# T3 on GpSimd, S's sums moved, the second sum split: a modulated 1-D convolution chain

## The chip, the cores and the metric

The kernel runs on one core of a Trainium2 chip. The metric is the device time of one execution in microseconds; the median of the runs is taken. The engines are TensorE (PE in the profile), VectorE (DVE), ScalarE (ACT), GpSimd (POOL) and SyncE (SP), which issues most of the DMAs.

## The reference

128 samples, each with 64 channels and 1024 positions, pass through four layers of a convolution with three taps whose weights depend on the sample. The layers are "same", "upsample", "same" and "downsample" with a fixed blur, there is no nonlinearity between them, and the input is added at the end.

```python
def _layer(x, style, w, b, mw, mb, typ):
    s = style @ mw.T + mb
    weight = SCALE * w * s[:, None, :, None]
    demod = lax.rsqrt(jnp.sum(weight * weight, axis=(2, 3)) + EPS)
    weight = weight * demod[:, :, None, None]
    if typ == 'same':
        out = jax.vmap(_conv_same)(x, weight) + b[None, :, None]
    elif typ == 'upsample':
        out = jax.vmap(_conv_up)(x, weight.transpose(0, 2, 1, 3)) + b[None, :, None]
        out = _blur(out, 2.0 * blur_k, (1, 1))
    elif typ == 'downsample':
        xb = _blur(x, blur_k, (2, 2))
        out = jax.vmap(_conv_down)(xb, weight) + b[None, :, None]
    return out
for i, typ in enumerate(('same', 'upsample', 'same', 'downsample')):
    out = _layer(out, style, weights[i], biases[i], mod_w[i], mod_b[i], typ)
x = x + out
```

## The kernel before

Since nothing nonlinear stands between the layers, the kernel multiplies the four weights of a sample into one filter of nine taps and runs that over the sample once. The three positions at either end, where the borders count, are computed apart and spread over the loop as one-off work.

Four samples (two pairs, of which one half lies on the upper and one on the lower 64 partitions) make one iteration q, 32 in all. The filter of nine taps over three planes (positions modulo three) is done with five products in place of nine taps by nine: conv0 to conv4 on TensorE, each 12 matmuls of 340 columns in float32. Their moving operands are sums of planes of the input X: T0 and T4 (`in04`, VectorE), T1 and T2 (`in1`, `in2`; one tile T12, made by GpSimd in the steady loop, lines L727 and L732 of the profile), T3 (`in3`, L712). T1, T2, T0 and T4 come from a tile G that VectorE makes with `in_g2` and `in_g01` (L663 with G in its name). Their weights are W (three stages of small matmuls) and H, sums of taps of W (`combine_a`, `combine_b`, `residual`: L663 with H, L660).

The products go into PSUM: conv3, then conv1 and conv2, then conv0 into psA(q), and conv4 into a bank pair Y that is one for all iterations. Between them stand sums on VectorE: `sum1` (y from psA and m3, a copy of conv3's result that ACT makes), `sum2` (Y = 3 m3 + psA after conv2, then y minus psA). conv4 adds onto Y, so it follows the first step of `sum2`.

The weights of later iterations are made in the same loop: `stage1` makes S(q+4), `stage2` makes R(q+2) with a scaled copy by ACT (table C), `stage3_b` and `stage3_a` make W(q+2). In the iterations 5 to 27 a part of stage2 is shared (`share`): it needs sums on S (`share_sums`, L463). The last group of `stage3_b` needs sums on R (`r_sums`, L589). Both are one `tensor_add` of 128 x 256 on VectorE with both inputs in SBUF.

The schedule is written out by hand: each engine gets its instructions in the order in which the functions are called, and semaphores are set between engines where data is handed on. `early_turn` writes iterations 0 to 3, `turn_of` 4 to 28 (4 is the entry, with an order of its own), and straight code the last three. In `turn_of(q)`, n is q+1, c is q+2 and s is q+4; its first half ends before conv4(q), its second half belongs to the time from conv4(q) to conv4(q+1). `EXTRA` holds the one-off work by iteration (`small_rest`, `var_newton`, tables on GpSimd in 5 and 7, and from 8 on `setup_x`, `rest0`, `rest1`, `rest1_bias`, `rest2` and `blur_side` on VectorE), `SLOTS` one-off matmuls in 9, 12, 14 and 19.

X has two buffers. SP's queue issues the six loads of an iteration (`load`, L146) and the stores of the outputs (`store`, L834) in the order of the calls; a load waits until the readers of its buffer are done.

Of the kernel before, what the change touches and what calls it, by code (L numbers as in the profile page):

```python
# [63 lines left out]
def kernel(  # L64
# [18 lines left out]
    nc_v, nc_a, nc_g = nc.vector, nc.scalar, nc.gpsimd  # L83
# [57 lines left out]
    def load(q, planes=slice(0, 3)):  # L141

        if q < NQ:
            at = slice(planes.start * PL, planes.stop * PL)
            for c in range(2):
                nc.sync.dma_start(Xs[q % NX][:, c, at], x[2 * q + c, :, at])  # L146
# [17 lines left out]
    def unit(pool, name):  # L164

        if pool is ps_w:
            return [pool.tile([P, 512], F32, tag=f"u{r}", name=f"{name}_{r}") for r in range(2)]
        t = pool.tile([P, 2, 512], F32, tag="u", name=name)
        return [t[:, r, :] for r in range(2)]


    NB = 340
    Y = ps_y.tile([P, 2, 512], F32, name="Y")
# [287 lines left out]
    def share_sums(q):  # L461
        t = whole[q]
        nc_v.tensor_add(t[:, :, 6:8], t[:, :, 1:5:3], t[:, :, 2:6:3])  # L463
# [92 lines left out]
    def new_w(q):  # L556
        Wq[q] = (
            wf_pool.tile([P, 9, 2, C], F32, tag="Wf", name=f"Wf{q}"),
            wf_pool.tile([P, 3, K, 2, C], F32, tag="H", name=f"H{q}"),
        )  # L560
# [5 lines left out]
    def blocks(ps, at):  # L566
        return [b.rearrange("c (a o) -> c a o", o=C)[:, at, :] for b in ps]

    def same_row(dst, weight, t, slots, first=False, last=False):
        for r, rows in enumerate(HALF):  # L570
            for c, cols in enumerate(HALF):
                nc.tensor.matmul(  # L572
                    dst[r][cols],
                    weight[rows],
                    t[rows, c, slots, :],
                    start=first,
                    stop=last,
                    skip_group_check=True,
                )

    def stage3_out(q, ps, at, n, engs=(nc_a, nc_a)):
        W = Wq[q][0]
        for r in range(2):
            src = ps[r][:, : n * C].rearrange("c (a o) -> c a o", o=C)
            scaled_copy(engs[r], W[:, at : at + n, r], src, t0[:, q, r : r + 1])

    def r_sums(q):
        t = chain[q]
        nc_v.tensor_add(t[:, :, 7:9], t[:, :, 2:6:3], t[:, :, 3:7:3])  # L589
# [38 lines left out]
    def stage3(q, part, pool=None, engs=(nc_a, nc_a)):  # L628

        t = chain[q]  # L630
        ps = unit(pool or ps_w, f"psW{q}_{part}")
        if part == 0:
            new_w(q)
        kinds = ((0, 1), (2,))[part]
        n = 0
        for i, kind in enumerate(kinds):
            for k in range(K):
                gs = [g for g in range(K) if 0 <= K * g + kind - k < 7]
                lo, m = gs[0], len(gs)
                first = K * lo + kind - k  # L640
                n += 1
                step = len(kinds)
                at = slice(i + step * lo, i + step * (lo + m - 1) + 1, step)
                same_row(
                    blocks(ps, at),
                    w0s[kind][:, k, :],
                    t,
                    slice(first, first + K * (m - 1) + 1, K),
                    n == 1,
                    n == K * len(kinds),  # L650
                )
        stage3_out(q, ps, *((3, 6), (0, 3))[part], engs)
        return ps
# [8 lines left out]
    def sum_of(out, x, f, y, op=ALU.add):  # L662
        nc_v.scalar_tensor_tensor(out, x, f, y, op0=ALU.mult, op1=op)  # L663
# [6 lines left out]
    def combine_a(q):  # L670

        chain.pop(q)
        a, b, c, h1, h2, h3 = taps(q)
        sum_of(h1, c, -2.0, a)
        residual(q)
        sum_of(h3, h1, 1.0 / 6.0, b)
# [9 lines left out]
    NJ = NB + 2  # L686
# [4 lines left out]
    BOTH_PAIRS = slice(0, 2)  # L691
    PAIR = slice(0, 1), slice(1, 2)

    def plane(buf, i, pairs=BOTH_PAIRS):

        at = PL * (2 - i) if i < 3 else PL * 2 + 1
        return buf[:, pairs, at : at + NJ]

    def t_tile(q, tag):
        if (q, tag) not in Ts:  # L700
            Ts[q, tag] = tpool.tile([P, 2, 1 + (tag != "T3"), PL], F32, tag=tag, name=f"{tag}_{q}")
        return Ts[q, tag]
# [3 lines left out]
            Gs[q] = gpool.tile([P, 2, 3 * PL], F32, tag="G", name=f"G{q}")  # L706
        return Xs[q % NX], Gs[q]

    def in3(q, pairs=BOTH_PAIRS):
        if q < NQ:  # L710
            X, t = Xs[q % NX], t_tile(q, "T3")
            nc_v.tensor_sub(t[:, pairs, 0, :NJ], plane(X, 3, pairs), plane(X, 1, pairs))  # L712

    def in_g01(q, pairs=BOTH_PAIRS):
        if q < NQ:
# [27 lines left out]
    def product(q, m, ps, groups=range(K)):  # L743

        W, H_ = Wq[q]
        tag, i = SLOT[m]
        for g in groups:
            for s, rows in enumerate(HALF):
                for c, cols in enumerate(HALF):
                    if m in (0, 4):  # L750
                        w = W[rows, tap(m // 2, g), c, :]
                    else:
                        w = H_[rows, m - 1, g, c, :]
                    nc.tensor.matmul(  # L754
                        ps[s][cols, :NB],
                        w,
                        Ts[q, tag][rows, c, i, g : g + NB],
                        start=(g == 0 and m == 3),
                        stop=(g == K - 1),
                        skip_group_check=True,  # L760
                    )
# [4 lines left out]
    m3c, y1w = {}, {}  # L766

    def parts(q):

        if isinstance(A[q], list):  # L770
            return [(slice(s, s + 1), A[q][s][:, None, :NB]) for s in range(2)]
        return [(slice(0, 2), A[q][:, :, :NB])]

    def banks(q):
        return A[q] if isinstance(A[q], list) else [A[q][:, s] for s in range(2)]
# [3 lines left out]
    def open_a(q):  # L779
        A[q] = ps_conv.tile([P, 2, 512], F32, tag="u", name=f"psA{q}")  # L780
        return banks(q)
# [22 lines left out]
    def conv2(q, *groups):  # L804
        product(q, 2, banks(q), groups or range(K))

    def sum2(q, steps=(0, 1)):
        for s, a in parts(q) if 0 in steps else ():
            sum_of(Y[:, s, :NB], m3c.pop(q)[:, s], 3.0, a)
        for s, a in parts(q) if 1 in steps else ():  # L810
            nc_v.tensor_sub(y1w[q][:, s], y1w[q][:, s], a)  # L811

    def conv4(q, *groups):
        product(q, 4, Y_banks, groups or range(K))

    def conv0(q, *groups):
        product(q, 0, banks(q), groups)
# [453 lines left out]
    def extra(*at):  # L1271
        EXTRA.get(at, lambda: None)()
# [4 lines left out]
    def sharing(q):  # L1277
        return FIRST < q < NQ - 4
# [105 lines left out]
    def turn_of(q):  # L1384
        n, c, s = q + 1, q + 2, q + 4
        entry = q == FIRST
        stage2(c)
        r_sums(c)
        if not entry:
            conv2(q)  # L1390
        sum2(q)
        if entry:
            conv4(q)
        stage3_b(c, open_a(n))
        combine_a(n)
        if entry:
            conv0(q, 0, 1)
        else:
            conv4(q)
        stage3_a(c)  # L1400
        combine_b(n)
        conv3(n)
        if entry:
            copy_m3(n)
        outputs(q, 2)
        for i in range(3):
            load(c + 1, slice(i, i + 1))
        if s < NQ:
            stage1_a(s)
        else:  # L1410
            slot(ends3, 3, unit(ps_w, "psE"), 3)
        if not entry:
            copy_m3(n)
        in04(n)
        in3(c)
        if q in SMALL:
            l, bs = SMALL[q]
            nc_v.memset(high(bs.stop - bs.start), 0.0)
        in_g2(c)
        conv0(q, *((2,) if entry else range(K)))  # L1420
        if entry:
            conv1(n, 0, 1)
        outputs(q, 1)
        if s < NQ:
            stage1_b(s)
            in_g01(c)
        else:
            rest3()
        if sharing(q):
            share(c + 1, banks(q))  # L1430
            share_copy(c + 1)
        outputs(q, 0)
        if q in SLOTS:
            slot(*SLOTS[q], Y_banks)
        if q in SMALL:
            small(q)
        conv1(n, *((2,) if entry else range(K)))
        sum1(n)
        if s == NQ:
            in_g01(c)  # L1440
        if sharing(q + 1):
            share_sums(s)
        in1(c, nc_g)
        in2(c, nc_g)
        for i in range(3):
            extra(q, i)
        if s + 1 < NQ:
            scale3(s + 1)

# [5 lines left out]
    q, n, c = NQ - 3, NQ - 2, NQ - 1  # L1455
    stage2(c)
    conv2(q)
    stage3(c, 0)
    sum2(q, (0,))
    combine_a(n)  # L1460
# [28 lines left out]
    q, n = NQ - 2, NQ - 1  # L1489
# [21 lines left out]
    q = NQ - 1  # L1511
# [89 lines left out]
```

## Time and profile before

| | |
|---|---|
| median of 3 runs | 511.38 us (509.64 to 512.12) |
| profiled execution | 514.02 us, of which the span is 512.2 us |
| mean granted TensorE clock | 0.989 |
| PE / DVE / ACT / POOL busy | 94% / 86% / 61% / 29% |
| instructions | 26699 |

The profile is of one execution. "Busy" is the union of an engine's instructions; a line gives its source line, the tiles it writes and reads, how often it ran, and in brackets the idle time of its engine just before it with what ended that. L663 is a helper (`sum_of`), so its rows are told apart by tiles. A row of a stretch of time gives the busy time and count of PE, PEld, DVE, ACT and POOL in it, then the granted clock, the DMA share and GB/s. L754 rows are two records per matmul.

### The profile page before, as it was taken

What the parts mean: (1) busy time and instruction counts of PE and PEld (TensorE: products, weight loads), DVE (VectorE), ACT (ScalarE), POOL (GpSimd) and SP (SyncE); (2) the same over time, 40 slices, a digit from 0 to 9 for tenths busy, and PEclk for the clock granted to TensorE, in tenths of its full rate; (3) what the DMA queues carried; (4) which work ended last, traced back from release to release, by engine and by line L of the source; (5) the groups of instructions that cost most, each with busy time, mean ns of one, the idle gap of its engine ahead of it and who ended that gap; (6) DMA issues with size and microseconds to landing.
All of it is one profiled execution on the core that took longest, in us unless ns stands there. A gap on an engine that the chain in (4) does not pass through costs nothing. (4 is left out here: it accounts for less than half of the span.)

```text
span 512.2 us, 26699 instructions
## 1 busy us (share of the span) xinstructions
PE 481.8 (94%) x11928; PEld 372.7 (73%) x11928; DVE 441.3 (86%) x684; ACT 313.3 (61%) x718; POOL 147.3 (29%) x173
## 2 busy tenths in 40 slices
PE   8999999898999999899999999999999999999975
PEld 7877888566997766776798767789666666688732
DVE  5799987679899889997979999869999999887784
ACT  5566577265666567556667665667665676765422
POOL 2433341333134322132333222333122333212200
PEclk9999999899899999999999999999999999999989
DMA  7207363055244455334554433455344555434514
GB/s 238 86 24 243 110 232 107 9 167 167 79 140 136 152 169 153 87 125 142 167 168 160 127 107 131 150 167 160 100 135 130 150 169 165 134 118 130 168 58 164
DMA packets 50499, 70.72 MB, mean 138 GB/s; under 512 B 5648, under 2 KB 47312, under 8 KB 50384
## 3 DMA queue, kind: packets, MB, share of 16 engines
q1 hardware_dynamic: 49792, 68.32, 42.4%
q8 instruction: 94, 1.54, 1.3%
q10 hardware_dynamic: 592, 0.69, 0.4%
q14 instruction: 21, 0.17, 0.1%
HBM read 35.36 MB, written 33.62 MB: 135 GB/s over the span
## 5 line engine op out<-in xcount | busy, mean ns | idle before, releaser
L754 PE MATMUL psA<-T,H 64*64 64x340 f32 x2304 | 190.2, 449 | 3.4 <-DVE y L663 3.2
L754 PEld LDWEIGHTS psA<-T,H 64*64 64x64 f32 x2304 | 100.5, 134 | 45.1 <-issue 7.4
L446 POOL TENSOR_TENSOR S<-S 128x128 f32<-128x128 f32 x28 | 23.4, 835 | 230.3 <-ACT S L361 230.3
L663 DVE SCALAR_TENSOR_TENSOR G<-X 128x1376 f32<-128x1376 f32 (+2 forms) x65 | 78.8, 1215 | 0.2 <-DMA X<-in_x 0.2
L754 PE MATMUL Y<-T,Wf 64*64 64x340 f32 x768 | 65.0, 460 | 5.4 <-DVE Y L663 5.3
L727 POOL TENSOR_TENSOR T<-G 128x684 f32<-128x684 f32 x28 | 46.6, 1663 | 75.3 <-DVE G L663 53.4
L361 ACT ACTIVATE R<-psR,tC 128x448 f32<-128x448 f32 x63 | 36.6, 631 | 46.1 <-PE psR L468 26.2
L754 PE MATMUL psA<-T,Wf 64*64 64x340 f32 x768 | 64.5, 446 | 0.0
L361 ACT ACTIVATE psW<-psA 128x128 f32<-128x128 f32 x100 | 19.3, 268 | 70.0 <-PE psA L572 60.5
L361 ACT ACTIVATE Wf<-psW,t 128x256 f32<-128x256 f32 (+2 forms) x76 | 32.7, 480 | 30.6 <-PE psW L572 30.3
L741 DVE TENSOR_TENSOR T<-G 128x1368 f32<-128x1368 f32 (+1 forms) x33 | 50.6, 1537 | 0.0
L754 PEld LDWEIGHTS Y<-T,Wf 64*64 64x64 f32 x768 | 34.3, 135 | 22.3 <-DVE Y L663 8.9
L732 POOL TENSOR_TENSOR T<-G 128x684 f32<-128x684 f32 x28 | 50.1, 1789 | 0.0
L468 PE MATMUL psR<-S,E 64*64 64x64 f32 (+1 forms) x1472 | 48.4, 237 | 1.3 <-issue 1.3
L572 PEld LDWEIGHTS psA<-R,w0s 64*64 64x64 f32 x1000 | 36.4, 137 | 14.8 <-issue 8.3
L468 PEld LDWEIGHTS psR<-S,E 64*64 64x64 f32 x1472 | 42.1, 134 | 6.1 <-issue 1.8
L572 PE MATMUL psA<-R,w0s 64*64 64x64 f32 (+2 forms) x1000 | 38.4, 268 | 8.5 <-issue 6.4
L390 PEld LDWEIGHTS psS<-wd,w2n 64*64 64x64 f32 x1120 | 37.3, 133 | 11.2 <-ACT S L361 0.8
L754 PEld LDWEIGHTS psA<-T,Wf 64*64 64x64 f32 x768 | 32.5, 133 | 12.2
L829 ACT ACTIVATE o<-psA,tb,td 128x340 f32<-128x340 f32 x63 | 37.2, 651 | 6.4 <-PE psA L754 6.4
L663 DVE SCALAR_TENSOR_TENSOR y<-psA,m 128x680 f32<-128x680 f32 x32 | 27.7, 865 | 13.8 <-PE psA L754 7.5
L829 ACT ACTIVATE o<-Y,tb,td 128x340 f32<-128x340 f32 x63 | 36.7, 638 | 4.6 <-PE Y L754 3.9
(165 smaller groups left out, 883.3 us busy)
## 6 DMA issues: line engine op xcount, KB each, us to landing
out<-o SPq DMA_DIRECT2D x167, 170.0 KB, 4.3
X<-in_x SPq DMA_DIRECT2D x150, 172.0 KB, 3.8
X<-in_x SPq DMA_DIRECT2D x14, 516.0 KB, 5.4
out<-o SPq DMA_DIRECT2D x6, 510.0 KB, 5.8
out<-o SPq DMA_DIRECT2D x2, 340.0 KB, 2.7
Xe<-in_x_ends SPq DMA_DIRECT2D x1, 512.0 KB, 6.7
out<-o ACTq DMA_DIRECT2D x3, 170.0 KB, 3.9
par<-in_params SPq DMA_DIRECT2D x2, 192.0 KB, 3.4
```

Source lines behind the costliest of these rows:

```text
L361: nc_a.activation(dst, src, AF.Copy, scale=f)
L390: nc.tensor.matmul(ps[r][cols, at * C : (at + n) * C], weight[rows], wd[c if r == 0 else 1 - c][rows, taps], start=first, stop=last, skip_ ...
L446: nc_g.tensor_add(t[:, :, 2], t[:, :, 2], t[:, :, 0])
L468: nc.tensor.matmul(dst[r][cols], weight[rows], st[c if r == 0 else 1 - c][rows, slots, :], start=False, stop=last, skip_group_check=True,)
L572: nc.tensor.matmul(dst[r][cols], weight[rows], t[rows, c, slots, :], start=first, stop=last, skip_group_check=True,)
L663: nc_v.scalar_tensor_tensor(out, x, f, y, op0=ALU.mult, op1=op)
L727: eng.tensor_add(t[:, :, 0, :NJ], plane(g, 2), plane(g, 1))
L732: eng.tensor_sub(t[:, :, 1, :NJ], plane(g, 2), plane(g, 1))
L741: nc_v.tensor_sub(t[:, pairs, :, :NJ], both(a, PL), both(b, 1))
L754: nc.tensor.matmul(ps[s][cols, :NB], w, Ts[q, tag][rows, c, i, g : g + NB], start=(g == 0 and m == 3), stop=(g == K - 1), skip_group_check ...
L829: nc_a.activation(dst, src, AF.Identity, bias=add, scale=d3)
```

## The change

- `in3` gets an engine, and the steady loop makes T3(n) on GpSimd in the iteration whose conv3(n) reads it; before, VectorE made T3(c) one iteration earlier. T3(30) is made on GpSimd as well; T3(31) stays on VectorE.
- The loads of X(c+1) are issued at the head of the iteration, behind T3(n), which is the last reader of that buffer; before, behind the stores of conv4's output.
- `share_sums(c+1)` stands behind `in04(n)` and ahead of `in_g2(c)`, in the iteration that uses it; before, `share_sums(s)` stood behind `sum1` in the iteration ahead.
- The first step of `sum2` is two instructions, one for each PSUM bank of Y.
- In the entry iteration `sum2(q)` and conv4(q) stand ahead of `r_sums(c)`.
- The one-off work stands ahead of `in1` and `in2`, which changes the order on GpSimd.

```diff
--- before.py
+++ after.py
@@ -706,10 +706,10 @@
             Gs[q] = gpool.tile([P, 2, 3 * PL], F32, tag="G", name=f"G{q}")
         return Xs[q % NX], Gs[q]
 
-    def in3(q, pairs=BOTH_PAIRS):
+    def in3(q, pairs=BOTH_PAIRS, eng=nc_v):
         if q < NQ:
             X, t = Xs[q % NX], t_tile(q, "T3")
-            nc_v.tensor_sub(t[:, pairs, 0, :NJ], plane(X, 3, pairs), plane(X, 1, pairs))
+            eng.tensor_sub(t[:, pairs, 0, :NJ], plane(X, 3, pairs), plane(X, 1, pairs))
 
     def in_g01(q, pairs=BOTH_PAIRS):
         if q < NQ:
@@ -805,8 +805,10 @@
         product(q, 2, banks(q), groups or range(K))
 
     def sum2(q, steps=(0, 1)):
-        for s, a in parts(q) if 0 in steps else ():
-            sum_of(Y[:, s, :NB], m3c.pop(q)[:, s], 3.0, a)
+        if 0 in steps:
+            m3 = m3c.pop(q)
+            for s, a in enumerate(banks(q)):
+                sum_of(Y[:, s, :NB], m3[:, s], 3.0, a[:, :NB])
         for s, a in parts(q) if 1 in steps else ():
             nc_v.tensor_sub(y1w[q][:, s], y1w[q][:, s], a)
 
@@ -1385,12 +1387,17 @@
         n, c, s = q + 1, q + 2, q + 4
         entry = q == FIRST
         stage2(c)
-        r_sums(c)
-        if not entry:
+        if entry:
+            sum2(q)
+            conv4(q)
+            r_sums(c)
+        else:
             conv2(q)
-        sum2(q)
-        if entry:
-            conv4(q)
+            r_sums(c)
+            sum2(q)
+            in3(n, eng=nc_g)
+        for i in range(3):
+            load(c + 1, slice(i, i + 1))
         stage3_b(c, open_a(n))
         combine_a(n)
         if entry:
@@ -1403,8 +1410,6 @@
         if entry:
             copy_m3(n)
         outputs(q, 2)
-        for i in range(3):
-            load(c + 1, slice(i, i + 1))
         if s < NQ:
             stage1_a(s)
         else:
@@ -1412,7 +1417,8 @@
         if not entry:
             copy_m3(n)
         in04(n)
-        in3(c)
+        if sharing(q):
+            share_sums(c + 1)
         if q in SMALL:
             l, bs = SMALL[q]
             nc_v.memset(high(bs.stop - bs.start), 0.0)
@@ -1438,12 +1444,10 @@
         sum1(n)
         if s == NQ:
             in_g01(c)
-        if sharing(q + 1):
-            share_sums(s)
+        for i in range(3):
+            extra(q, i)
         in1(c, nc_g)
         in2(c, nc_g)
-        for i in range(3):
-            extra(q, i)
         if s + 1 < NQ:
             scale3(s + 1)
 
@@ -1455,6 +1459,7 @@
     q, n, c = NQ - 3, NQ - 2, NQ - 1
     stage2(c)
     conv2(q)
+    in3(n, eng=nc_g)
     stage3(c, 0)
     sum2(q, (0,))
     combine_a(n)
```

## The prediction

> **What bounds the kernel now.** I read the head of the page first (what each engine is busy with), then the groups of instructions by line, then the timeline of one iteration, then the waits of TensorE. Iteration q is counted from the first matmul of conv4(q) to that of conv4(q+1).
>
> ```profile
> span 512.2 us, 26699 instructions
> PE 481.8 (94%) x11928; PEld 372.7 (73%) x11928; DVE 441.3 (86%) x684; ACT 313.3 (61%) x718; POOL 147.3 (29%) x173
> ...
> L712 DVE TENSOR_TENSOR T<-X 128x684 f32<-128x684 f32 x32 | 27.6, 864 | 0.0
> L463 DVE TENSOR_TENSOR S<-S 128x256 f32<-128x256 f32 x23 | 28.9, 1258 | 0.0
> L589 DVE TENSOR_TENSOR R<-R 128x256 f32<-128x256 f32 x25 | 11.5, 461 | 14.8 <-ACT R L361 14.7
> L732 POOL TENSOR_TENSOR T<-G 128x684 f32<-128x684 f32 x28 | 50.1, 1789 | 0.0
> ```
>
> TensorE is busy 94% of the span, VectorE 86%. The two lines L463 (the sums on S) and L589 (the sums on R) are the same instruction on the same shape, 256 elements a partition; one takes 1258 ns and the other 461. Iteration 24 shows why.
>
> ```profile
> 406.21 1.95 PE L754 MATMUL Y<-T,Wf 64*64 64x340 f32 x24 [0.33 <-DVE Y L663]
> 413.26 0.61 DVE L443 SCALAR_TENSOR_TENSOR S<-psS,tB,S 128x128 f32<-128x128 f32 x2 [0.17 <-PE psS L390]
> 413.78 1.58 DVE L663 SCALAR_TENSOR_TENSOR G<-X 128x1376 f32<-128x1376 f32 x1
> ...
> 415.35 0.86 DVE L663 SCALAR_TENSOR_TENSOR y<-psA,m 128x680 f32<-128x680 f32 x1
> 415.53 1.68 POOL L727 TENSOR_TENSOR T<-G 128x684 f32<-128x684 f32 x1 [2.13 <-DVE G L663]
> 416.14 1.35 DVE L463 TENSOR_TENSOR S<-S 128x256 f32<-128x256 f32 x1
> 417.14 1.85 POOL L732 TENSOR_TENSOR T<-G 128x684 f32<-128x684 f32 x1
> 417.24 1.16 ACT L361 ACTIVATE R<-psR,tC 128x448 f32<-128x448 f32 x2 [0.84 <-PE psR L468]
> 417.41 2.60 DVE L1071 TENSOR_TENSOR Ue<-Ve 128x448 f32<-128x448 f32 x2
> 419.56 0.49 PE L572 MATMUL psA<-R,w0s 64*64 64x64 f32 x16
> 419.93 0.41 DVE L589 TENSOR_TENSOR R<-R 128x256 f32<-128x256 f32 x1
> 420.26 0.86 DVE L663 SCALAR_TENSOR_TENSOR Y<-m,psA 128x680 f32<-128x680 f32 x1
> 420.39 0.45 PE L572 MATMUL psA<-R,par 64*64 64x128 f32 x8 [0.35 <-DVE R L589]
> 421.18 1.09 PE L754 MATMUL Y<-T,Wf 64*64 64x340 f32 x12 [0.33 <-DVE Y L663]
> ```
>
> GpSimd's first T12 operation runs from 415.53 to 417.21. The sums on S are asked for at 416.14 and end at 417.49, 0.28 after it. GpSimd's second operation ends at 418.99, 1.50 after the sums, and the two L1071 steps, begun at 417.41, end at 420.01, 1.02 after that. So a VectorE step with two SBUF inputs and a GpSimd operation that reads SBUF run one at a time, and they take turns. The y sum at 415.35 and the Y sum at 420.26, with an input in PSUM, keep 0.86 whatever GpSimd does.
>
> The rest of the iteration is paced by TensorE: before L443 VectorE idles 0.17 for the psS matmuls. The chain that TensorE waits for at the end is G sum (end 415.36), GpSimd, VectorE steps, sums on R, Y sum (end 421.12), conv4 (421.18), with TensorE idle for R and again for Y. This stretch decides the change.
>
> **The change, part by part.** T3 leaves VectorE: 0.864 us an iteration (row L712). That is worth nothing by itself, since it stands ahead of the 0.17 wait for psS: VectorE only waits longer there. S's sums move to the same place, cost about 0.41 there, and that is hidden by the same wait. T3 lands on GpSimd behind the two T12 operations, in the very stretch shown above; the trace has no T3 there, but T12 has its shape (684 elements), so it is priced at one port turn, 1.50, and at most 1.79 (row L732). Below, if it found the port free, it costs nothing.
>
> ```profile
> 172.29 2.73 DVE L973 TENSOR_TENSOR Xm<-Xe,sc 128x512 f32<-128x512 f32 x2
> 206.00:209.00 3.00, 1.27 (x52) 1.15 (x50) 2.97 (x6) 0.00 (x0) 0.00 (x0) 1.00 0.05 14
> 481.06 0.56 DVE L663 SCALAR_TENSOR_TENSOR H<-H,Wf 128x384 f32<-128x384 f32 x1
> ```
>
> With one-off steps on VectorE between the y sum and the sums on R (L1071 here) the turns now go, on iteration 24's times: first T12 to 417.21; first step 0.48 to 417.69; second T12 to 419.19; second step 0.48 to 419.67 (I halve the 1.02, less the pipelining); T3 1.50 to 421.17; sums on R 0.28 to 421.45. It was 420.34. The Y sum is split: 680 elements take 0.86 and 384 take 0.56 (481.06), so 340 take 0.50, and the second half waits for the first (it does in the changed program's instruction list, about 0.03), so 1.03 for 0.86. conv4 waits for the second half in that list, so nothing starts sooner and 0.17 is added. Y ends at 422.40 instead of 421.12, and conv4 comes 1.28 later. Such iterations are 8, 10, 11, 13, 15, 16, 17 and 20 to 24, twelve in all; first and last are L973 (172.29) and L1071 above. Iteration 9 has twelve small steps and I count it too. Where the steps are shorter the rise is a little less: 13 x 1.2 = 15.6. In iteration 10 TensorE is idle 1.73 there already (3.00 less 1.27 in the stretch from 206), until after Y has ended, which hides 0.9. **+14.7.**
>
> ```profile
> 325.26 1.85 POOL L732 TENSOR_TENSOR T<-G 128x684 f32<-128x684 f32 x1
> 326.35 1.16 ACT L361 ACTIVATE R<-psR,tC 128x448 f32<-128x448 f32 x2 [1.82 <-PE psR L468]
> 327.54 0.43 DVE L589 TENSOR_TENSOR R<-R 128x256 f32<-128x256 f32 x1 [1.94 <-ACT R L361]
> ```
>
> Without such steps the sums on R are asked for while the second T12 runs, get the next turn, and T3 follows harmlessly: no change. But in iteration 18 R lands at 327.51, after the second T12 (327.11 here, 0.18 sooner without S's sums). T3 then goes first, to 328.45, and the sums end at 328.73 instead of 327.97: **+0.9** with the split. In 12, 14 and 19 R comes later still and only the split counts, +0.1 each: **+0.3**.
>
> **Iteration 3 to 4.** The Y sum stood behind the sums on R, and those behind ACT; conv4 stood behind the Y sum.
>
> ```profile
> 91.52 1.16 ACT L361 ACTIVATE R<-psR,tC 128x448 f32<-128x448 f32 x2 [2.17 <-PE psR L534]
> 92.71 0.46 DVE L589 TENSOR_TENSOR R<-R 128x256 f32<-128x256 f32 x1 [4.15 <-ACT R L361]
> 94.01 3.55 PE L754 MATMUL Y<-T,Wf 64*64 64x340 f32 x24 [2.46 <-DVE Y L663]
> ...
> 94.00:97.00 3.00, 2.99 (x24) 1.50 (x28) 2.93 (x7) 0.00 (x0) 0.31 (x1) 0.53 0.00 0
> ...
> PE psA L572 <- ACT R L361: 2.1, 1, 2.1
> ```
>
> VectorE idles 4.15 there, so the Y sum now fits into that wait and conv4 follows stage2 at once: 2.46 saved. The idle time also cost clock: granted 0.53 in the next 3 us, conv4 3.55 long for 1.95 usually (406.21), 1.60 more saved. What covers it is that conv4 hides ACT's R (1.16) and the sums on R (0.46). In iteration 4 the three GpSimd operations wait for c0f, which now stands ahead of them, so the H sums meet T3: between 0 and one port turn, I take 0.6. **-3.5.**
>
> A rule weighed here: the Trainium skill, TensorE: Matmul & The Clock Gate, "HAM oscillation", gives "no PE-idle gaps >~3.4µs". The trace is stricter: 2.46 was enough, 1.73 (206 to 209, clock 1.00) was not. By the rule the term for the clock below is nil and the sum +16.9; by the row it is not.
>
> **Iterations 5 to 8.** The one-off work on GpSimd now goes ahead of T12.
>
> ```profile
> 126.92 0.69 POOL L288 TENSOR_TENSOR tC<-dm 64x48 f32<-64x48 f32 x2 [0.78 <-DVE dm L258]
> 129.84 0.39 POOL L883 TENSOR_TENSOR Da<-sc,dm 128x96 f32<-128x96 f32 x1
> 129.00:131.00 2.00, 2.00 (x49) 2.00 (x52) 2.00 (x4) 0.00 (x0) 1.15 (x3) 0.50 0.00 0
> ...
> 158.81 0.85 POOL L285 TENSOR_SCALAR tb<-oc 64x48 f32<-64x48 f32 x2 [0.15 <-DVE oc L930]
> 161.23 0.43 POOL L959 MEMSET g<- 128x384 f32 x1
> ...
> 478.57 1.65 POOL L732 TENSOR_TENSOR T<-G 128x684 f32<-128x684 f32 x1
> 479.33 1.30 DVE L663 SCALAR_TENSOR_TENSOR H<-Wf 128x384 f32<-128x384 f32 x1
> 480.56 0.47 DVE L660 SCALAR_TENSOR_TENSOR Wf<-idn,t,Wf 128x64 f32<-128x64 f32 x2
> ...
> 481.67 1.95 PE L754 MATMUL psA<-T,H 64*64 64x340 f32 x24
> ```
>
> Iteration 5: table C came behind T12, ACT's R waited for it and TensorE for R, 2.1, with the clock at 0.50 behind it (some 1.2 more): 3.3 saved. But tables and vectors (tC to Da, 126.92 to 130.23, 3.3 us) now push both T12 and T3 onto the H sums of iteration 6. The row at 479.33 shows an H sum under a T12: 1.30 for 0.56. On those times the first H sum meets the first T12 some 0.35 before its end, one residual step waits for the second T12 and the other for T3: 0.35 + 1.50 + 1.50, less 0.25 of their own start, 3.1 in all. I take 0.3 as the slack that H has (0.05 at 481.67), so TensorE waits 2.8 at conv3(7), and by the row of 2.46 loses the clock, 1.4: 4.2 against 3.3, **+0.9**. Iteration 7: tb to the last memset (158.81 to 161.66) do the same to conv3(9), with no gain against it: **+2.0** (0 to 3.5).
>
> **The end.** In iteration 28 GpSimd's T3(30) follows the T12 that ends at 480.22. The H sum gets its turn, then the residual waits one turn of 1.4 to 1.5, and conv3(30), which starts 0.05 after that chain, moves with it; VectorE is the bound until the 2.99 stall at 490.79, so it is not won back: **+1.4**, and **+0.2** for two split sums behind.
>
> **The clock.** In the thirteen iterations TensorE idles from 420.05 (L572's end) to 421.45, works 0.45, and idles 0.56: 2.0 in 2.4. That lies between 1.73 (no loss) and 2.46 (loss of 1.6). None to all of thirteen may lose about 1.4: 0 to 18; nearer to 1.73, I take two: **+2.8**.
>
> Loads and stores: the loads wait for T3 in SP's queue, with the stores of conv4's output behind them, which come some 3.5 after conv4's start, when T3 has long ended; the data is used an iteration later. Nothing.
>
> Sum: 14.7 + 0.9 + 0.3 - 3.5 + 0.9 + 2.0 + 1.4 + 0.2 + 2.8 = +19.7, put at 20. The profiled execution took 514.02 with its 512.2 span, 1.8 around it; the median of the runs is 511.38, 2.6 below that execution, and I add the difference to it: **531.4**. Its own range is 522 to 538.
>
> **The rivals.** *Faster, GpSimd gives way.* If T3, behind semaphore waits of its own for the loads, asks for the port only after the sums on R, each of thirteen iterations gains 0.2 instead (S's sums gone, split added: -2.9 in all), and the H collisions lose T3's 1.5 each: +0.9 becomes -0.6, +2.0 becomes 0.5, the end's 1.4 nothing. With -3.5 for iterations 3 and 4 and +0.5 for splits that is -6.0, 505.4. It decides when T3's dispatch takes longer than a VectorE step (0.48). For it: VectorE issues densely. Against it: at 417.14 the second T12 got its turn ahead of the L1071 step already in line. The Trainium skill, SBUF — State Buffer, "Who interferes with whom", has the shared pair as an exclusive lock taken by whoever comes first; by it the faster rival hangs on dispatch alone. Chance 0.12.
>
> *VectorE is the bound.* Then 0.86 and 0.8 of blocking, less 0.17, come off 21 iterations, 31 us; TensorE's idle time, 512.2 less 481.8, caps that at 30: 481.4. Against it: the idle 0.17 before L443. Chance 0.04.
>
> *The clock falls in all thirteen.* 18.2 for 2.8: 546.8. For it: 2.0 idle in 2.4 is close to the 2.1 that lost it at 129. Chance 0.12.
>
> **How the numbers follow.** The forecast keeps 0.72. The range runs from 510, which leaves out VectorE as the bound and most of the giving way, to 546, just short of the clock falling everywhere. A difference of 0.5% (2.6 us) is about what can be told from no change: faster 0.13, the same 0.05, slower 0.82.
>
> **What would show it.** Right: L463 near 0.42; T3 on GpSimd right behind the second T12; in iterations 8 to 24 with one-off steps L589 at 1.2 or more and TensorE's wait for R up by about 1.2; L660 or L663 on H long in iterations 5 to 8 and 28; conv4(4) following stage2 without a gap. Wrong: L589 near 0.45 in those iterations, T3 running behind it. That is the faster rival. VectorE without idle before L443 would mean that the pace was misread.

## The result, and the profile after

| | before | after |
|---|---|---|
| median of the runs, same chip | 511.75 us (509.64 to 512.94, 4 runs) | 531.21 us (530.06 to 536.38, 4 runs) |
| profiled execution, its span | 514.02, 512.2 | 530.83, 529.0 |
| mean granted TensorE clock | 0.989 | 0.986 |

The change makes the kernel slower: the ratio is 1.0405, with a 95% interval of 1.0328 to 1.0481. The forecast was 531.4.

The head of the page and the groups by line, for the changed kernel (busy us, mean ns, idle before):

```profile
span 529.0 us, 26759 instructions
PE 483.3 (91%) x11928; PEld 345.5 (65%) x11928; DVE 443.7 (84%) x691; ACT 313.6 (59%) x718; POOL 191.0 (36%) x198
...
L463 DVE TENSOR_TENSOR S<-S 128x256 f32<-128x256 f32 x23 | 9.6, 418 | 0.0
L589 DVE TENSOR_TENSOR R<-R 128x256 f32<-128x256 f32 x25 | 27.7, 1107 | 21.4 <-ACT R L361 21.4
L712 POOL TENSOR_TENSOR T<-X 128x684 f32<-128x684 f32 x25 | 46.0, 1842 | 0.0
L732 POOL TENSOR_TENSOR T<-G 128x684 f32<-128x684 f32 x28 | 52.2, 1863 | 0.0
```

The cost has changed places. S's sums (L463) fell from 1258 to 418 ns, since GpSimd rests where they now stand. R's sums (L589), which nobody touched, rose from 461 to 1107 ns. VectorE is not relieved: 25 T3 operations went, and its busy time rose from 441.3 to 443.7 us, because time spent blocked counts as busy (16.2 us more for R's sums alone) and two sums for Y take 5.2 us more than one. TensorE's busy time rose by 1.5 us only, so nearly all of the 16.8 us by which the span grew is TensorE waiting. The waits of TensorE say for what (us in total, times, longest):

```profile
PE psA L572 <- DVE R L589: 19.4, 13, 1.9
PE psA L754 <- DVE H L663: 7.9, 4, 3.2
PE Y L754 <- DVE Y L663: 7.7, 15, 0.5
...
PE psA L572 <- issue: 0.5, 2, 0.3
```

The wait for R was 2.3 us before. The timeline of iteration 23 in the changed kernel, from G's last sum to the next conv4, shows how it comes about (rows of the chain alone):

```profile
413.56 1.58 DVE L663 SCALAR_TENSOR_TENSOR G<-X 128x1376 f32<-128x1376 f32 x1
415.31 1.67 POOL L727 TENSOR_TENSOR T<-G 128x684 f32<-128x684 f32 x1 [2.58 <-DVE G L663]
415.92 3.67 DVE L1073 TENSOR_TENSOR Ve<-Ue 128x512 f32<-128x512 f32 x2
416.92 2.11 POOL L732 TENSOR_TENSOR T<-G 128x684 f32<-128x684 f32 x1
419.00 2.07 POOL L712 TENSOR_TENSOR T<-X 128x684 f32<-128x684 f32 x1
419.51 1.85 DVE L589 TENSOR_TENSOR R<-R 128x256 f32<-128x256 f32 x1
421.27 1.05 DVE L663 SCALAR_TENSOR_TENSOR Y<-m,psA 128x340 f32<-128x340 f32 x2
421.41 0.45 PE L572 MATMUL psA<-R,par 64*64 64x128 f32 x8 [1.66 <-DVE R L589]
422.38 1.98 PE L754 MATMUL Y<-T,Wf 64*64 64x340 f32 x12 [0.53 <-DVE Y L663]
```

R's sums are issued at 419.51, while T3 (L712) holds the shared reads, and end at 421.36, 0.29 after T3's end at 421.07. Without T3's reads they take 0.41, as the run without those reads shows below. TensorE's matmuls on R stand idle for 1.66, and conv4 for another 0.53 until the second bank of Y is summed.

### The profile page after: what moved, and what is told of

It is laid out like the page before. It is cut to its first block, busy times and chain, and to the rows that moved or that the text cites. A ratio compares the mean times of both kernels' runs of the same rounds, so it can differ in the third digit from the quotient of the medians.

```text
span 529.0 us, 26759 instructions
## 1 busy us (share of the span) xinstructions
PE 483.3 (91%) x11928; PEld 345.5 (65%) x11928; DVE 443.7 (84%) x691; ACT 313.6 (59%) x718; POOL 191.0 (36%) x198
## 5 line engine op out<-in xcount | busy, mean ns | idle before, releaser
L754 PE MATMUL psA<-T,H 64*64 64x340 f32 x2304 | 185.4, 447 | 11.0 <-DVE H L663 7.9
L754 PEld LDWEIGHTS psA<-T,H 64*64 64x64 f32 x2304 | 86.8, 133 | 62.1 <-POOL T L712 7.7
L446 POOL TENSOR_TENSOR S<-S 128x128 f32<-128x128 f32 x28 | 19.6, 701 | 200.8 <-ACT S L361 200.8
L754 PE MATMUL Y<-T,Wf 64*64 64x340 f32 x768 | 68.5, 488 | 7.8 <-DVE Y L663 7.7
L754 PEld LDWEIGHTS Y<-T,Wf 64*64 64x64 f32 x768 | 30.2, 141 | 31.7 <-DVE Y L663 12.5
L712 POOL TENSOR_TENSOR T<-X 128x684 f32<-128x684 f32 x25 | 46.0, 1842 | 0.0
L468 PE MATMUL psR<-S,E 64*64 64x64 f32 (+1 forms) x1472 | 45.7, 237 | 0.0
L589 DVE TENSOR_TENSOR R<-R 128x256 f32<-128x256 f32 x25 | 27.7, 1107 | 21.4 <-ACT R L361 21.4
L390 PEld LDWEIGHTS psS<-wd,w2n 64*64 64x64 f32 x1120 | 33.8, 133 | 14.8 <-ACT S L361 0.8
L468 PEld LDWEIGHTS psR<-S,E 64*64 64x64 f32 x1472 | 38.1, 134 | 5.5
L831 ACT ACTIVATE o<-y,tb,td 128x340 f32<-128x340 f32 x62 | 38.6, 679 | 0.6 <-DVE y L813 0.6
```

The costliest lines, as they stand in the source:

```text
L390: nc.tensor.matmul(ps[r][cols, at * C : (at + n) * C], weight[rows], wd[c if r == 0 else 1 - c][rows, taps], start=first, stop=last, skip_ ...
L446: nc_g.tensor_add(t[:, :, 2], t[:, :, 2], t[:, :, 0])
L468: nc.tensor.matmul(dst[r][cols], weight[rows], st[c if r == 0 else 1 - c][rows, slots, :], start=False, stop=last, skip_group_check=True,)
L712: eng.tensor_sub(t[:, pairs, 0, :NJ], plane(X, 3, pairs), plane(X, 1, pairs))
L754: nc.tensor.matmul(ps[s][cols, :NB], w, Ts[q, tag][rows, c, i, g : g + NB], start=(g == 0 and m == 3), stop=(g == K - 1), skip_group_check ...
L831: nc_a.activation(dst, src, AF.Identity, bias=add, scale=d3)
```

## The experiments

In each set the kernel before ran on the same chip. "The stretch" below is the time from the end of G's last sum to the start of the next conv4, and "the 13" are the iterations 8 to 11, 13, 15 to 17 and 20 to 24, which carry one-off VectorE steps.

### T3 back on VectorE

```diff
-            in3(n, eng=nc_g)
...
         in04(n)
+        in3(c)
```

> Of the changed kernel, T3 alone is put back: made by VectorE behind the T0/T4 sum, one iteration ahead; loads, S's sums, split, entry and one-off order stay. Port theory (T3 holds the port that the sums on R need): L589's mean back from 1107 to under 500 ns, TensorE's wait for R from 19.4 to under 6 us, each of the 13 iterations 1.5 shorter (19.5), some 3 off the H collisions, most of the half-clock stretches gone (5): about 503 us. Rival, the split and the new order cost the time: 525 or more with L589 still short of a change in TensorE's wait for Y. Rival, VectorE is the bound and gets 0.86 back an iteration: above 531.

Measured: 506.69 us, ratio 0.9898 (0.9866 to 0.9930). In twelve of the 13 the stretch fell from between 6.7 and 7.4 us to between 5.2 and 5.9 (in iteration 9 from 9.0 to 7.5), and none of them was followed by a conv4 at half clock, where four were in the changed kernel. The group of R's sums and TensorE's wait for them:

```profile
L589 DVE TENSOR_TENSOR R<-R 128x256 f32<-128x256 f32 x25 | 14.4, 576 | 20.1 <-ACT R L361 20.0
...
PE psA L572 <- DVE R L589: 4.7, 11, 0.6
```

So T3's move alone accounts for the loss; all the other parts together gain some 5 us. One figure was missed: the mean of R's sums is 576 ns for the 500 expected, since R is ready earlier in iterations such as 18 and 25 to 27 and its sums then meet T2 (0.97 us in 25). And of the collisions with H in iterations 6 and 8 little went: from conv4 to the end of G's last sum they still take 11.8 and 11.5 us (12.5 and 12.0 with T3 on GpSimd, 9.6 and 9.5 in the kernel before), so most of what they cost is not T3's. The run also shows what T3 costs on VectorE now: conv4 to the end of G's last sum takes 9.49 us instead of 9.15, 0.34 of T3's 0.86.

### T3 written by GpSimd without reading the planes

```diff
-            eng.tensor_sub(t[:, pairs, 0, :NJ], plane(X, 3, pairs), plane(X, 1, pairs))
+            if eng is nc_g:
+                for _ in range(3):
+                    eng.memset(t[:, :, 0, :NJ], 0.0)
+                eng.tensor_copy(t[:, :, 0, :1], X[:, :, :1])
+            else:
+                eng.tensor_sub(t[:, pairs, 0, :NJ], plane(X, 3, pairs), plane(X, 1, pairs))
```

T3's values are left out here.

> Of the changed kernel, GpSimd fills T3 with constants three times in place of the difference, then copies one column of X (so that the loads keep their wait); the output is not the reference's. GpSimd stays as long busy, but reads almost nothing from SBUF. Port theory (only a GpSimd operation that reads SBUF holds up a VectorE step with two SBUF inputs): L589 under 600 ns, TensorE's wait for R under 6 us, time about 503 to 508. Rival, it is GpSimd's time or its place in the queue that counts: L589 stays near 1.1 us, time 528 to 533.

Measured: 506.83 us, ratio 0.9942 (0.9903 to 0.9980). Groups by line of this kernel (the second row is T3 in its place), then the timeline of iteration 23:

```profile
L589 DVE TENSOR_TENSOR R<-R 128x256 f32<-128x256 f32 x25 | 12.7, 507 | 22.2 <-ACT R L361 22.1
L714 POOL MEMSET T<- 128x684 f32 x75 | 50.2, 670 | 2.9
...
401.31 2.12 POOL L714 MEMSET T<- 128x684 f32 x3
401.84 0.41 DVE L589 TENSOR_TENSOR R<-R 128x256 f32<-128x256 f32 x1
```

GpSimd is busy for 2.12 us in T3's slot, longer than T3 took, and R's sums run in its midst in 0.41. The time understates this, since TensorE waited for these fills themselves in three places (7.6 us). What blocks is not a busy GpSimd but one that reads SBUF. The Trainium skill, SBUF — State Buffer, "Who interferes with whom", says that a VectorE instruction with two SBUF inputs contends with a GpSimd instruction that reads SBUF and not with one that only writes it; the two rows of R's sums in iteration 23, 1.85 beside a T3 that reads and 0.41 beside one that only writes, agree.

### The loads late again, and the loads early in the kernel before

In the changed kernel:

```diff
-        for i in range(3):
-            load(c + 1, slice(i, i + 1))
         stage3_b(c, open_a(n))
...
         outputs(q, 2)
+        for i in range(3):
+            load(c + 1, slice(i, i + 1))
```

In the kernel before, the reverse.

> Of the changed kernel, the loads alone are put back behind the stores of conv4's output. Theory A, the early loads are why TensorE's idle time 'issue' fell from 9.6 to 1.0 us: it comes back to 5 or more, and the time rises by 2 to 5, to 533 to 536. Theory B, it went because TensorE waits elsewhere for longer: it stays at 1, and the time at 531. The sums on R stay at 1.1 us in both.

> The kernel before, whole, with one thing of the change: the three pieces of load(c + 1) stand ahead of stage3_b instead of behind outputs(q, 2). Nothing is left out. Theory A (the idle that TensorE's rows put down to issue, 9.6 us before and 1.0 after, comes from the place of the loads): the issue idle falls to about 1 us, iterations 18, 25 and 26 shorten by 0.8 to 1.3 us each, iterations 8 to 17 by up to 0.5 each where R stood behind that idle, and the time falls by 4 to 6 us against the kernel before, to about 505. Theory B (the idle comes from what else the change moves, S's sums or the one-off steps, and the early loads only went with it): the issue idle stays at 8 to 10 us and the time stays within 1 us of the kernel before.

Measured: 535.55 us, ratio 1.0486 (1.0434 to 1.0537) for the changed kernel with late loads; 509.05 us, ratio 0.9961 (0.9931 to 0.9991) for the kernel before with early ones. Waits of TensorE, with late loads first, then with early loads in the kernel before ("issue" is idle time for which the profile shows nothing that ended it):

```profile
PE psA L572 <- DVE R L589: 12.5, 10, 1.9
PE psA L572 <- issue: 5.4, 5, 1.5
PE psR L468 <- issue: 3.2, 4, 1.8
```

```profile
PE Y L754 <- DVE Y L663: 7.0, 15, 2.5
PE psA L572 <- DVE R L589: 6.2, 10, 0.8
...
PE psA L572 <- issue: 1.0, 2, 0.6
```

The kernel before has 7.5 us of such idle at L572 and 1.6 at L468. The idle goes and comes with the place of the loads. What it is worth is less than its length: of the 8 us that it fell, the kernel before kept 4.7 in the profile and 2.0 (0.5 to 3.5) by the runs, where 4 to 6 were expected, while its wait for R rose from 2.3 to 6.2 and that for Y from 5.3 to 7.0. What TensorE waits for there was not tried by a run, but the traces hold it:

```profile
207.85 0.54 PE L572 MATMUL psA<-R,w0s 64*64 64x128 f32 x10 [1.73 <-issue]
q8 instruction: 1, 0.02, 2.5%
```

The second row is from the DMA queues in the stretch from 204 to 206.5: one 16 KB piece of program. In the kernel before this queue fetches 94 such pieces, about one for every 256 of TensorE's 24008 matmuls and weight loads. All 78 such idle times above 0.2 us in the 14 profiles of this case end at a matmul 193 or 194 places past a multiple of 256 in that order, and 1.2 to 1.6 us after a piece has landed. So TensorE waits for its own instructions. In the kernel before, the DMA engines were at least 85% busy in the 2 us ahead of the 16 pieces that it waited for, and 33% in the mean ahead of the others; that late loads hold up a piece by filling the DMA engines is inferred from this.

### One sum for Y again, and two sums in the kernel before

```diff
-        if 0 in steps:
-            m3 = m3c.pop(q)
-            for s, a in enumerate(banks(q)):
-                sum_of(Y[:, s, :NB], m3[:, s], 3.0, a[:, :NB])
+        for s, a in parts(q) if 0 in steps else ():
+            sum_of(Y[:, s, :NB], m3c.pop(q)[:, s], 3.0, a)
```

> Of the changed kernel, the Y sum is one instruction again. Theory: conv4 waited for the second half, so 0.2 an iteration goes where TensorE waits for Y (15 iterations), and 0.5 in the first three: 531 to about 528; TensorE's wait for Y from 0.53 to 0.33 each. Rival, the halves let TensorE start sooner: 531 or more.

> The kernel before with one thing of the change: Y's sum made bank by bank, two instructions of 128x340 instead of one of 128x680. Nothing is left out. Theory A (two sums end 0.2 us later than one, and this counts wherever the second convolution's sum is what conv4 waits for): conv4's wait for Y rises by 0.2 us at 12 to 25 places, VectorE carries 5 us more, and the time rises by 2 to 5 us, 0.4 to 1.0 per cent, with more where a stretch at half clock is set off. Theory B (the first bank's matmuls can start while the second is summed, and the later end is taken up by TensorE's other waits): the time stays within 1 us of the kernel before.

Measured: 531.84 us, ratio 1.0389 (1.0327 to 1.0451), for the changed kernel with one sum, and 515.43 us, ratio 1.0061 (1.0020 to 1.0102), for the kernel before with two. The group of Y's sums with two, to stand beside the 863 ns of one:

```profile
L663 DVE SCALAR_TENSOR_TENSOR Y<-m,psA 128x340 f32<-128x340 f32 x64 | 32.8, 513 | 7.0 <-PE psA L754 5.7
```

On the kernel before the split costs 3.1 us (1.0 to 5.2), as the first theory had it. The run without the split in the changed kernel decides nothing on time: Y's sums ended 0.2 us earlier everywhere, and TensorE's wait for Y fell from 7.7 to 4.7 us, but in that execution more iterations fell to half clock (granted mean 0.971, and 0.971 to 0.984 in its four runs), and the gain was lost there; the 528 expected was missed.

### R's sums on GpSimd

```diff
-        nc_v.tensor_add(t[:, :, 7:9], t[:, :, 2:6:3], t[:, :, 3:7:3])
+        nc_g.tensor_add(t[:, :, 7:9], t[:, :, 2:6:3], t[:, :, 3:7:3])
```

> The changed kernel with R's sums (line 589) made by GpSimd, so that T3 stands behind them in GpSimd's own queue: T1, T2, R's sums, T3. Nothing is left out. Theory A (the loss is R's sums waiting out GpSimd's T3 in the port's turns): R's sums start when T2 ends, 3.5 to 3.9 us behind G01's end, and end before conv2 does or within 0.5 us of it, in the 13 iterations with one-off steps too; the time from G01's end to conv4 there falls from 6.7 to 7.3 us to between 4.8 and 5.6 (R no longer waits for VectorE's one-off steps either), 1.4 to 2.2 us each, 18 to 28 us over 13 and another 3 to 6 where no half-clock stretch follows: 500 to 510 us. Theory B (GpSimd is itself slowed by VectorE's steps, so that its R sums come late too): T2 or R's sums stretch by a VectorE step of 2.1 us, the wait for R at the matmuls stays near 1.7 us in those iterations, and the time stays at 526 to 533.

Measured: 518.72 us, ratio 1.0154 (1.0083 to 1.0226). In twelve of the 13 the stretch fell to between 4.9 and 6.0 us, ten of them below 5.7, and no half-clock start followed, as the first theory had it. But the total misses the 500 to 510 expected, for a reason that neither theory named: iterations 4, 5 and 7 took 24.3, 20.2 and 18.1 us, against 17.1, 15.5 and 14.4 in the changed kernel, 15.5 more. The timeline of iteration 5 shows what they met:

```profile
130.81 0.39 POOL L885 TENSOR_TENSOR Da<-sc,dm 128x96 f32<-128x96 f32 x1
131.16 1.64 POOL L727 TENSOR_TENSOR T<-G 128x684 f32<-128x684 f32 x1
132.74 1.95 POOL L732 TENSOR_TENSOR T<-G 128x684 f32<-128x684 f32 x1
134.65 0.71 POOL L589 TENSOR_TENSOR R<-R 128x256 f32<-128x256 f32 x1
135.42 0.45 PE L572 MATMUL psA<-R,par 64*64 64x128 f32 x8 [4.06 <-POOL R L589]
```

R's sums are last in a queue that begins with the one-off tables, so TensorE waits for them there (12 waits, 16.9 us in all).

### The one-off steps behind T1 and T2 again

```diff
+        in1(c, nc_g)
+        in2(c, nc_g)
         for i in range(3):
             extra(q, i)
-        in1(c, nc_g)
-        in2(c, nc_g)
```

> The changed kernel with the one-off steps issued behind T1 and T2 again, as in the kernel before; nothing else. Nothing is left out. Theory A (the waits of matmuls for H in iterations 6 and 8 come from T1 and T2 standing behind GpSimd's one-off work in iterations 5 and 7): G01's end to conv4's start of the same iteration falls from 12.5 to 9.5 or 9.9 in iteration 6 and from 12.0 to 9.5 in iteration 8, iteration 5 gives back between 0 and 3.3 us, in sum 2 to 5.3 us less than the changed kernel: 526 to 529. The 13 iterations with one-off steps keep their 6.7 to 7.3 us, since the steps there are VectorE's. Theory B (these waits come from T3 on GpSimd or from S's sums): they stay, and the time stays within 1 us of the changed kernel.

Measured: 528.50 us, ratio 1.0348 (1.0264 to 1.0432), 2.9 us below the changed kernel by the two ratios, though their intervals overlap. The waits for H:

```profile
PE psA L754 <- DVE H L663: 1.8, 2, 1.4
```

They were 7.9 in four, the longest 3.2. Iteration 6 fell from 17.4 to 14.6 us; iteration 8 only from 19.2 to 18.0, since with its wait for H gone conv3(9) waited 1.02 for ACT's copy of W, and iteration 5 gave back 0.9. The 13 kept their stretch of 6.7 to 7.4.

### The entry alone

```diff
-        r_sums(c)
         if not entry:
+            r_sums(c)
             conv2(q)
         sum2(q)
         if entry:
             conv4(q)
+            r_sums(c)
```

> The kernel before with one thing of the change: in the entry iteration Y's sums and conv4 stand ahead of R's sums. Nothing is left out. Theory A (the prediction's step on the entry, 3.5 net of a wait for H): iteration 3 falls from 18.0 to 15.3 us, iteration 4 from 19.4 to about 17.2, in sum 4 to 5 us less in the profile, part of which a later wait for H of up to 0.9 gives back: 0.6 to 1.0 per cent below the kernel before, 506 to 509 us. Theory B (the entry's gain in the changed kernel came from S's sums or the loads there): iterations 3 and 4 keep 36.5 to 37.4 us in sum and the time does not change.

Measured: 507.40 us, ratio 0.9865 (0.9806 to 0.9925), a gain of 6.9 us (3.9 to 10.0). In the profile iterations 3 and 4 took 15.27 and 17.71 us for 18.00 and 19.40, 4.4 less, and the span was 4.1 below that of before. The timeline at that place:

```profile
89.58 0.87 DVE L663 SCALAR_TENSOR_TENSOR Y<-m,psA 128x680 f32<-128x680 f32 x1 [0.53 <-PE psA L754]
91.77 1.97 PE L754 MATMUL Y<-T,Wf 64*64 64x340 f32 x24
93.20 0.47 DVE L589 TENSOR_TENSOR R<-R 128x256 f32<-128x256 f32 x1 [1.99 <-ACT R L361]
```

conv4 follows at full clock, and R's sums run beneath it.

### Put together

Three kernels keep the early loads, the entry's order, S's sums in their new place and one sum for Y, and put R's sums on GpSimd. In the first they are there throughout, and iteration 7 alone has its one-off steps behind T1 and T2. In the second and third GpSimd makes them from iteration 8 on, where its queue is free of one-off work, and all one-off steps stand behind T1 and T2; the third has T3 back on VectorE. The edit to R's sums in these two:

```diff
+        eng = nc_g if q >= 11 else nc_v
-        nc_v.tensor_add(t[:, :, 7:9], t[:, :, 2:6:3], t[:, :, 3:7:3])
+        eng.tensor_add(t[:, :, 7:9], t[:, :, 2:6:3], t[:, :, 3:7:3])
```

> The changed kernel with R's sums on GpSimd ahead of T3, one sum for Y over both banks, and in iteration 7 alone the one-off steps behind T1 and T2. Nothing is left out. Theory A: as for R's sums on GpSimd alone, and 0.2 us less at each of some 25 conv4 starts where Y is last, and 2.4 us less in iteration 8: 494 to 505 us, below both kernels. Theory B (GpSimd's R sums late, or a new wait for T3 behind them): 520 us or more, no better than the kernel before.

> The changed kernel with R's sums on GpSimd, ahead of T3 in its queue, from iteration 8 on only (VectorE makes them in iterations 4 to 7, where GpSimd has one-off work of its own), all one-off steps behind T1 and T2 again, and one sum for Y over both banks. Nothing is left out. Theory A (what the mixed kernel lost against 500 us lay in iterations 4, 5 and 7, where GpSimd's R sums stood behind its one-off work): iterations 4 to 7 take 62 to 63 us, as with the one-off steps behind T1 and T2, instead of 76.6, iterations 10 to 28 stay at 14 to 16 each, and the time is 498 to 503 us, below the kernel before by 1.5 to 2.5 per cent. Theory B (GpSimd's R sums need the one-off steps ahead of T1 and T2, or the loss of iterations 4 to 7 has another cause, such as T3 there): 508 us or more.

> The same kernel as the mixed one with GpSimd's R sums from iteration 8 on, but with T3 made by VectorE at its old place behind in04. Nothing is left out. Theory A (what is won comes from R's sums ahead of VectorE's one-off steps, from the early loads and the entry, and T3 on GpSimd gains nothing more): VectorE carries 21 us more, G01 ends 0.1 to 0.3 later in an iteration, but the first combination of H after R's sums (mean 754 ns against 566 where GpSimd's T3 runs beside it) is back at 566, so the time is within 3 us of the same kernel with T3 on GpSimd, 498 to 505. Theory B (VectorE bounds the iteration once R's wait is gone, so T3's 0.86 us each count in full): 15 us or more above that kernel, 513 to 520.

Measured: 514.12 us, ratio 1.0040 (1.0008 to 1.0072); 502.12 us, ratio 0.9776 (0.9725 to 0.9827); 499.30 us, ratio 0.9714 (0.9670 to 0.9757). The first misses the 494 to 505 expected: it spent 76.6 us in iterations 4 to 7, and the second 63.0, which settles where R's sums on GpSimd lost. The second and the third beat both kernels. Iteration 24 of the third, and the combinations of H from W with T3 on GpSimd (second kernel) and on VectorE (third):

```profile
405.43 3.62 DVE L1072 TENSOR_TENSOR Ue<-Ve 128x448 f32<-128x448 f32 x2
406.51 2.05 POOL L733 TENSOR_TENSOR T<-G 128x684 f32<-128x684 f32 x1
408.52 1.10 POOL L590 TENSOR_TENSOR R<-R 128x256 f32<-128x256 f32 x1
409.68 0.45 PE L572 MATMUL psA<-R,par 64*64 64x128 f32 x8 [0.64 <-POOL R L590]
```

```profile
L664 DVE SCALAR_TENSOR_TENSOR H<-Wf 128x384 f32<-128x384 f32 x64 | 48.1, 751 | 0.0
```

```profile
L664 DVE SCALAR_TENSOR_TENSOR H<-Wf 128x384 f32<-128x384 f32 x64 | 36.7, 574 | 0.0
```

R's sums start as T2 ends, while the one-off steps are still under way, and TensorE waits 0.64 for them, where it waited 1.53 in the changed kernel's iteration 24. T3 on GpSimd gains nothing even when R's sums stand ahead of it (502.12 against 499.30, intervals that overlap): part of what VectorE saves it loses in its combinations of H, which then run beside T3.

## Why the prediction was right, by its own steps

The time and the main mechanism were right; some terms missed and offset each other.

- **The 13 iterations, +14.7.** The stretch grew by 15.1 us: 1.1 to 1.4 in twelve, and 0.33 in iteration 10, where an idle TensorE hid most, as forecast. The turns came as worked out: iteration 24 was put at 1.28 more and had 1.29 (5.82 to 7.11).
- **Iteration 18, +0.9.** Wrong in sign: 14.71 became 13.91. The step that failed was "Loads and stores: Nothing". The early loads took away the idle that made R late, so R was ready 3.04 us after G's last sum instead of 4.03, ahead of T3. With the loads late again R came at 3.69, behind T2's end at 3.45, T3 went first, and the iteration took 15.52, 0.8 above before. The same idle, TensorE's wait for its program, vanished in 7, 25 and 26 (-0.56, -1.27, -0.89), which nothing in the sum foresaw.
- **12, 14 and 19, +0.3.** The stretch grew by 0.24.
- **Entry, -3.5.** Iterations 3 and 4 lost 5.0 us and gave 0.9 back in a wait for H in iteration 5, so -4.1; the kernel with the entry's order alone shows -4.4 without that wait.
- **Iterations 5 to 8, +0.9 and +2.0.** The collision came as told. In the changed kernel conv3(7) stood still:

```profile
126.30 3.24 DVE L660 SCALAR_TENSOR_TENSOR Wf<-idn,t,Wf 128x64 f32<-128x64 f32 x2
127.83 1.63 POOL L712 TENSOR_TENSOR T<-X 128x684 f32<-128x684 f32 x1
130.28 1.95 PE L754 MATMUL psA<-T,H 64*64 64x340 f32 x24 [3.15 <-DVE H L663]
```

  The stall was 3.15 for the 2.8 predicted, and iteration 8 had one of 2.4 for the 2.0. Against it iteration 5 won 3.3 us in its stretch, as predicted; 5 and 6 together came to -0.4 without the entry's share, for the +0.9. The step that failed is the 1.4 of clock behind the stall: the clock stayed full there.
- **The end, +1.4 and +0.2.** The stall of 1.40 came at 499.13, in iteration 29 as counted here, but it was won back in the same iteration: the stall near its end was 2.81 for 2.99, and it did not cost the clock this time, so that the two convolutions behind it took 3.66 for 5.00. Iterations 28 and 29 together changed by -0.1. "Not won back" was the wrong step, and only by the clock: without it some 1.2 of the 1.4 would have stayed, an estimate from these rows.
- **The clock, +2.8.** Mis-sized: four of the 13 lost it, in iterations 10, 12, 21 and 24 behind them, 1.6 to 1.7 us each, 6.6 in all. The reasoning by the length of the idle also fell. Here are the conv4 at 405.99, which kept the clock, and the one at 422.38, which lost it (the column before the DMA share is the granted clock):

```profile
405.01 0.45 PE L572 MATMUL psA<-R,par 64*64 64x128 f32 x8 [1.85 <-DVE R L589]
401.95:405.36 3.41, 1.56 (x60) 1.26 (x52) 3.41 (x3) 0.00 (x0) 2.72 (x2) 1.00 0.02 6
405.36:408.78 3.42, 2.89 (x64) 1.90 (x64) 3.32 (x9) 1.62 (x6) 0.00 (x0) 1.00 0.71 202
419.02:422.43 3.41, 1.23 (x52) 0.85 (x44) 3.38 (x5) 0.45 (x3) 2.05 (x2) 1.00 0.11 20
422.43:425.84 3.41, 3.41 (x26) 1.57 (x30) 3.31 (x8) 1.17 (x4) 0.00 (x0) 0.50 0.60 194
```

  The idle of 1.85 and 0.53 kept the clock, the shorter one of 1.66 and 0.53 lost it. The stretches shown are chosen by the trace's record of the clock: within the changed kernel's execution it changes only at times that lie whole multiples of 3.413 us apart (193.74, 197.15, 227.87, 231.28, 371.23, 374.64, 422.43, 425.84). What counts is TensorE's idle time within one stretch of that grid. From 419.02 to 422.43 both idle times fall into one stretch, 2.18 in all, and the next runs at half clock; at 405.36 the grid parts them, 1.85 and 0.53, and the clock stays. At the 13 places the four that lost it had 1.90 to 2.18 in one stretch and the nine others 1.85 at most. The stall of 3.15 in iteration 6 was parted into 1.76 and 1.40, the one of 2.81 at the end into 1.09 and 1.72. In the 14 profiles, by the matmuls on record, no stretch with less than 1.59 of idle lost the clock and none with more than 1.93 kept it; between the two both occur. The grid does not start with the program (its first change comes at 9.42 here and at 8.86 in the kernel before), so how many of the 13 lose the clock was a matter of chance for the prediction. The rule weighed in the prediction, idle gaps of no more than some 3.4 us from the Trainium skill, TensorE: Matmul & The Clock Gate, "HAM oscillation", is not borne out here either. By it the 1.4 behind iteration 6's stall of 2.8 would have gone from the sum as well, so that it was 15.5 by that rule and not 16.9.
- **The rivals.** In the 13, T3 did not give way to R's sums, VectorE was not the bound and the clock did not fall everywhere. The early rows asked for, L463 near 0.42 and a raised wait for R, are there; L589 at 1.2 or more in the 13 is too (1.85) except in 9, 16 and 17, where all of T3 ran beside the step ahead and R's sums only started later (in iteration 16 at 5.75 for 4.87).

Luck had a part. The sum of 19.7 is made from a profile, and between the two profiles the span grew by 16.8, 2.9 less: behind the 13 the clock cost 3.8 more than the sum held and in iteration 6 it cost 1.4 less, while iteration 18, the idle that vanished in 7, 25 and 26, and the end gave back some 6. The medians differ by 19.5, because the profiled execution before lay 2.3 above its median and that of the changed kernel 0.4 below. So that 531.4 came within 0.2 of 531.21 is chance; that the time lies well inside the range, and why, is not.

## What to carry to other kernels

Before an operation goes to GpSimd, ask which VectorE step with two SBUF inputs will be issued while it runs, and whether someone waits for that step: the operation moved here saved VectorE nothing and put 1.2 us on the path 13 times. GpSimd's order is a tool too: putting the awaited sums on GpSimd themselves, from the iteration on where its queue is free, with T3 left on VectorE, gave 2.9% less than the kernel before. Where a change has several parts, run each alone: here the entry's order and the early loads were gains, the split of Y's sum a small loss, and all were hidden beneath the loss from T3.

## What the runs showed of the hardware that was not expected

- The same pattern of TensorE idle time lost half the clock in 4 of 13 places, and a longer one kept it (2.38 us in two parts kept it, 2.19 lost it). The granted clock changed only on a grid of 3.413 us, and the idle time within one stretch of it decided: in the changed kernel 1.90 or more at those places lost the next stretch, 1.85 or less did not.
- TensorE's idle of 9.1 us that the profile puts down to "issue" (L572 and L468) followed the place of the DMA loads in the program: 0.5 with early loads, 8.6 with late ones in the same kernel. It is TensorE waiting for the next 16 KB of its program: all 78 such idle times end 193 or 194 places past a multiple of 256 of its matmuls and weight loads.
- A GpSimd operation that only fills memory, 2.12 us long, left a VectorE step with two SBUF inputs at its usual 0.41 us.
